# Sine angles in turns, a separate store for the first taps, and two issuers for the first Toeplitz loads

## The chip, the cores and the metric

The kernel runs on one core of one Trainium2 chip. The metric is the device time of the program in microseconds (us). The profile is of one execution of the program; its engines are called PE (TensorE, with PEld for its weight loads), DVE (VectorE), ACT (ScalarE), POOL (GpSimd) and SP (SyncE, which here only issues transfers).

## The reference, cut to what matters

Two layers run after one another on x of shape 4 x 64 x 256 x 256 (batch, channel, height, width), all in 32-bit floats.

```python
# layer 0: a long separable convolution; the filters come from small sine networks
h = sin(freq * (z @ w1 + b1))          # z: 256 positions x 33
h = sin(freq * (h @ w2 + b2))
h = sin(freq * (h @ w3 + b3))
h = (h @ wo) * decay                   # 256 taps for each of 64 channels; once for X, once for Y
k = outer product of hx and hy         # per channel
y = causal 2-D convolution of x with k # written with rfft2 of size 512
x = y + x * bias

# layer 1: whitening over the 64 channels
x1   = x as 64 x (4 * 256 * 256)
x1_s = x1[:, ::9]
cov  = x1_s @ x1_s.T / n + 0.01 * I
out  = newton_schulz_isqrt(cov, 5) @ (x1 - mean(x1_s))
```

The inputs are drawn so that the angles freq * (...) reach many turns: they have to be brought back into one turn before the sine is looked up.

## The kernel before, in words

**Filters.** The X and the Y network run together, as the two halves of 128 partitions (`wbd` holds block-diagonal weights). The 256 positions are split in two halves `u` of 128. In each of three layers `i`, a product of 128 x 128 (`pm`, L156) lands in PSUM; ACT evacuates it with scale `freq` and bias `bf` (L159); DVE brings the angle into one turn with five operations (L160 to L164: divide by 2 pi and round by adding and subtracting the constant MAGIC, take the turns off in two parts TP1 and TP2, clamp); ACT takes the sine (L165). The list `hs` feeds the next layer. After each layer's two halves, `busy(...)` puts filler products on zeros into the PE queue (L150; a call is two PE instructions, called passes in this text). A last product `pf` (L172) times `decay` (L173) gives `taps`, one row of 256 taps and 128 zeros for each of 128 filters.

**Taps to memory and back.** SP writes the first two rows to `g0_d` in memory (L174), ACT writes all 128 rows to `g_d` (L175). The Toeplitz matrix of a channel is a load in which each partition reads its row one element further on (`load_toeplitz`, L183 to L195). For the first group of 8 channels 14 such loads are issued by SP (L548 to L550), two for each piece of channels, one for each half of 64 partitions; the first pair reads `g0_d`, the rest `g_d`. The profile gives both memory tiles the name `g_d`.

**The convolution.** The work is 32 steps (a group of 8 channels of one image), each in four items of two channels. An item needs two products with Toeplitz matrices, first along one axis (read from x, copied out of PSUM to `o1`) and then along the other. `group` does the first stage of one item together with the second stage of the item two places earlier (L215, copies L399, bias L402), so the first two items run alone, in `half_group` (L247, copies L281). In it the two channels of an item begin on opposite halves of the partitions (`k = step ^ u`). Products that share row tiles are kept in order by no-operations on POOL, `fence`. Two steps ahead, SP loads x; it stores the result to `y_d` (L415), and loads further Toeplitz matrices at hand-set places (`blocks`), the first of them at step 0, c = 4. The order on every engine from here on is that of the code (`manual_schedule`).

**Sampling and whitening.** DVE packs every ninth element into `samp` (L314). The last image's last channels are packed by PE instead, with nine selection matrices `pick` (`pack_by_pe`), which POOL computes in the prologue from `ident` and `rows`, a cast of `mask` (L132 to L135). After the covariance and the Newton-Schulz steps, a second pass reads `y_d`, multiplies by the whitening matrix and writes `out` (L601 to L631).

The two writes and their fillers:

```python
    nc.sync.dma_start(out=g0_d, in_=taps[0:2])
    nc.scalar.dma_start(out=g_d, in_=taps)
    busy(20)
```

Of the kernel before, what the change touches and what calls it, by code (L numbers as in the profile page):

```python
# [37 lines left out]
F32 = mybir.dt.float32  # L38
I32 = mybir.dt.int32
AF = mybir.ActivationFunctionType  # L40
ALU = mybir.AluOpType
# [3 lines left out]
NB, C, L = 4, 64, 256  # L45
P, H2 = 128, 2
EMB, ORDER = 33, 64
PIX = L * L
CG = 8
HP = P // 2  # L50
STEP = 9
# [4 lines left out]
GW = P + L  # L56
FP = 4096


TP1 = 6.28125  # L60
TP2 = 2.0 * math.pi - TP1
MAGIC = 12582912.0


# [1 line left out]
def conv_whiten_kernel(ctx: ExitStack, tc: tile.TileContext, a: dict, out: bass.AP):  # L66
    nc = tc.nc
    x = a["x"]

    const = ctx.enter_context(tc.tile_pool(name="const", bufs=1))  # L70
# [5 lines left out]
    dram = ctx.enter_context(tc.tile_pool(name="dram", bufs=1, space=bass.MemoryType.DRAM))  # L76
# [1 line left out]

    y_d = [dram.tile([H2 * C, PIX // H2], F32, tag=f"y{n}", name=f"y_d{n}") for n in range(NB)]
    g_d = dram.tile([P, GW], F32, tag="g", name="g_d")  # L80
    g0_d = dram.tile([2, GW], F32, tag="g0", name="g0_d")

# [4 lines left out]
    cols = const.tile([P, 4], F32, tag="cols", name="cols")  # L89
    nc.scalar.dma_start(out=cols, in_=a["cols"])  # L90

    bf = const.tile([P, 3], F32, tag="bf", name="bf")
# [5 lines left out]
    mask = const.tile([P, NB, H2, STEP], I32, tag="mask", name="mask")  # L98
    bias = const.tile([P, C], F32, tag="bias", name="bias")

    def load_x(t, g, n, c):
        nc.sync.dma_start(
            out=t[:, c : c + 2],
            in_=x[n, g][:, c : c + 2],
        )
# [13 lines left out]
    ident = const.tile([P, P], F32, tag="ident", name="ident")  # L119
    make_identity(nc, ident)  # L120
    samp = []
    for n in range(NB):
        t = spool.tile([P, FP], F32, tag="samp", name=f"samp{n}")
# [5 lines left out]


    rows = const.tile([P, STEP], F32, tag="rows", name="rows")
    nc.gpsimd.tensor_copy(rows, mask[:, NB - 1, 0, :])  # L132
    pick = const.tile([P, STEP, P], F32, tag="pick", name="pick")
    for s in range(STEP):
        nc.gpsimd.tensor_scalar(pick[:, s, :], ident, rows[:, s : s + 1], None, ALU.mult)  # L135

    taps = scratch[:, 11:13, :].rearrange("p a w -> p (a w)")[:, 0:GW]
    nc.gpsimd.memset(taps[:, L:GW], 0.0)  # L140
    freq = cols[:, 3:4]
    nc.vector.tensor_scalar(bf, cols[:, 0:3], freq, None, ALU.mult)

    idle = o1pool.tile([P, H2 * L], F32, tag="o1", name="idle")
# [2 lines left out]
    def busy(times):  # L147
        p = psA.tile([P, P], F32, tag="psA", name="busy")
        for _ in range(times):
            nc.tensor.matmul(p, lhsT=idle[:, 0:P], rhs=idle[:, P : 2 * P], start=True, stop=True)  # L150

    hs, wt = [zw[:, u * P : (u + 1) * P] for u in range(2)], zw[:, L : L + P]
    for i in range(3):
        for u in range(2):
            pm = psA.tile([P, P], F32, tag="psA", name=f"pm{i}_{u}")
            nc.tensor.matmul(pm, lhsT=wt, rhs=hs[u], start=True, stop=True)  # L156
            half = slice(u * P, (u + 1) * P)
            arg, k, nxt = (scratch[:, 2 + 3 * i + v, half] for v in range(3))
            nc.scalar.activation(arg, pm, AF.Identity, bias=bf[:, i : i + 1], scale=freq)  # L159
            nc.vector.tensor_scalar(k, arg, 1.0 / (2.0 * math.pi), MAGIC, ALU.mult, ALU.add)  # L160
            nc.vector.tensor_scalar(k, k, MAGIC, None, ALU.subtract)
            for part in (TP1, TP2):
                nc.vector.scalar_tensor_tensor(arg, k, -part, arg, ALU.mult, ALU.add)  # L163
            nc.vector.tensor_scalar(arg, arg, 3.1415925, -3.1415925, ALU.min, ALU.max)  # L164
            nc.scalar.activation(nxt, arg, AF.Sin)  # L165
            hs[u] = nxt
        wt = wbd[:, i * P : (i + 1) * P]
        busy((5, 10, 9)[i])
    for u in range(2):
        half = slice(u * P, (u + 1) * P)  # L170
        pf = psA.tile([P, P], F32, tag="psA", name=f"pf{u}")
        nc.tensor.matmul(pf, lhsT=wt, rhs=hs[u], start=True, stop=True)  # L172
        nc.vector.tensor_tensor(taps[:, half], pf, decay[:, half], ALU.mult)  # L173
    nc.sync.dma_start(out=g0_d, in_=taps[0:2])  # L174
    nc.scalar.dma_start(out=g_d, in_=taps)  # L175
    busy(20)

    def new_toeplitz(g):


        return tpool.tile([P, 2, CG, L], F32, tag="toep", name=f"toep_{g}")

    def load_toeplitz(t, g, f, half, lo=0, hi=CG):  # L183
        source, row = (g0_d, 0) if (g, f, lo) == (0, 0, 0) else (g_d, f * C + g * CG + lo)


        skip = 0 if f == half else HP
        nc.sync.dma_start(
            out=t[half * HP : (half + 1) * HP, f, lo:hi, skip:],
            in_=bass.AP(  # L190
                tensor=source.tensor,
                offset=source.offset + row * GW + skip,
                ap=[[1, HP], [GW, hi - lo], [1, L - skip]],
            ),
        )  # L195
# [126 lines left out]
    def covariance(n):  # L322

        pc = psA.tile([P, C + 1], F32, tag="psA", name=f"pc{n}")
        for b in range(H2):
            for j in range(NJ):
                half = slice(C * (j % 2), C * (j % 2 + 1))
                nc.tensor.matmul(  # L328
                    pc[half],
                    lhsT=samp[n][:, b, j, 0:C],  # L330
                    rhs=samp[n][:, b, j, :],
                    start=(b == 0 and j < 2),
                    stop=(b == H2 - 1 and j >= NJ - 2),
                    skip_group_check=True,
                )
        nc.vector.scalar_tensor_tensor(cov, pc, 1.0 / NSAMP, cov, ALU.mult, ALU.add)  # L336
# [18 lines left out]
    def load_next():  # L355
        loaded[len(loaded)] = load_y(len(loaded))
# [10 lines left out]
    for g in range(1, C // CG):  # L367
        first = 16 * g - 14 if g < C // CG - 1 else 16 * g - 22
        for part in range(8):
            k = first + (part * 12 // 8 if g < C // CG - 2 else part)  # L370
# [7 lines left out]
    def pack(time=math.inf):  # L378
        while todo and time > 0:
            cost, op = todo.pop(0)  # L380
            op()
            time -= cost
# [160 lines left out]
    with tc.manual_schedule(  # L543
        engines={engines.PE, engines.SP, engines.DVE, engines.Activation, engines.Pool}
    ):
        toep = {0: new_toeplitz(0)}

        for f, lo, hi in ((0, 0, 2), (0, 2, 4), (0, 4, 6), (1, 0, 2), (0, 6, 8), (1, 2, 4), (1, 4, 8)):  # L548
            for half in range(2):
                load_toeplitz(toep[0], 0, f, half, lo, hi)  # L550
        for c in range(0, CG, 2):
            load_x(x_tiles[1], *steps[1], c)
        for i, (g, n) in enumerate(steps):
            xt = x_tiles[i % 4]
            for c in range(0, CG, 2):
                item = (g, n, c, xt, [])
                if g == C // CG - 1 and n > 0 and c == 4:
                    covariance(n - 1)
                if len(pending) == 2:
                    group(item, pending.pop(0))  # L560
                else:
                    half_group(item, 0)
                pending.append(item)
                if i == 0 and c == 6:

                    fold = const.tile([P, C], F32, tag="fold", name="fold")
                    nc.vector.tensor_tensor(fold, ident[:, 0:C], ident[:, C:P], ALU.add)

                    nc.scalar.activation(bf[:, 0:1], samp[0][:, 0, 0, C : C + 1], AF.Sqrt)

                if i + 2 < len(steps):
                    load_x(x_tiles[(i + 2) % 4], *steps[i + 2], c)
                if (i, c) in blocks:
                    tg, part = blocks[i, c]
                    if part == 0:
                        toep[tg] = new_toeplitz(tg)
                    lo = part % 2 * CG // 2
                    load_toeplitz(toep[tg], tg, part // 4, part // 2 % 2, lo, lo + CG // 2)
                for _ in range(early.get((i, c), 0)):
                    load_next()  # L580
        g, n, c, yt, _ = pending[0]
        for item in pending:
            half_group(item, 1)
            pack(1.0)
            store(item)

        pack()
        i15 = place(2 * C, rows=C).rearrange("p (u c) -> p u c", u=2)
        for u in range(2):
            nc.vector.tensor_scalar(i15[:, u], ident[0:C, 0:C], 1.5, None, ALU.mult)  # L590
        ones = place(P, rows=C)
        nc.gpsimd.memset(ones, 1.0)  # L592
        for lo in range(CG // 2, CG, 2):
            pack_by_pe(g, n, yt, slice(lo, lo + 2))
        covariance(NB - 1)
        while len(loaded) < len(homes):
            load_next()
        W, shift = whitening(i15, ones)
# [3 lines left out]
    for i, (n, q) in enumerate(pieces):  # L602
# [3 lines left out]
        part = FP if 1 < i < len(pieces) - 2 else FP // 4  # L606
        for w in range(FP // 1024):
# [5 lines left out]
            cols = [slice((2 * w + k) * 512, (2 * w + k + 1) * 512) for k in range(2)]  # L613
# [76 lines left out]
```

## Time and profile before

| what | value |
| --- | --- |
| median of 3 runs | 910.22 us (907.89 to 911.49) |
| profiled execution, its own time | 911.4 us |
| its span, first to last instruction | 909.6 us |
| mean granted PE clock | 0.951 |
| first product of the convolution that is followed by an unbroken stream | 19.44 us |
| POOL: nine picks | 5.46 us, from 11.80 |
| SP: 14 first Toeplitz loads | issued from 15.23 to 25.85 us |

A row of the page or of the timeline names line, engine, operation and tiles. In the timeline the first number is the start in us from the first instruction, the second the duration of the merged instructions, `x4` their number, and in brackets the idle time before them with what ended it. In the chain of waits there are start, duration and what the time was spent on; "issue" is time in which the engine waited for nothing that is shown, `SPq` SP's queue. A row of the table by stretch gives the stretch, its length, the busy time (and the number of instructions) of PE, PEld, DVE, ACT and POOL, then the granted PE clock, the mean busy share of the 16 DMA engines and GB/s.

### The profile page before, as it was taken

What the parts mean: (1) busy time and instruction counts of PE and PEld (TensorE: products, weight loads), DVE (VectorE), ACT (ScalarE), POOL (GpSimd) and SP (SyncE); (2) the same over time, 40 slices, a digit from 0 to 9 for tenths busy, and PEclk for the clock granted to TensorE, in tenths of its full rate; (3) what the DMA queues carried; (4) which work ended last, traced back from release to release, by engine and by line L of the source; (5) the groups of instructions that cost most, each with busy time, mean ns of one, the idle gap of its engine ahead of it and who ended that gap; (6) DMA issues with size and microseconds to landing.
All of it is one profiled execution on the core that took longest, in us unless ns stands there. A gap on an engine that the chain in (4) does not pass through costs nothing.

```text
span 909.6 us, 28286 instructions
## 1 busy us (share of the span) xinstructions
PE 792.2 (87%) x11928; PEld 636.7 (70%) x11928; DVE 657.6 (72%) x882; ACT 479.8 (53%) x798; POOL 31.4 (3%) x71
## 2 busy tenths in 40 slices
PE   8999999999999999999999999999977777775500
PEld 7999999999999999999999999998411111111100
DVE  3368786878687868876787766767699999996500
ACT  2545454545454545555555544541598888885400
POOL 3000000000000000000000000000110000000010
PEclk9999999999999999999999999998999999996655
DMA  4998788797888788878987898879899999999998
GB/s 154 303 305 261 250 243 263 251 276 247 253 262 265 247 255 267 263 249 253 297 282 234 285 400 323 290 253 386 346 383 433 428 432 429 428 433 428 432 430 342
DMA packets 117550, 285.61 MB, mean 314 GB/s; under 512 B 8973, under 2 KB 91312, under 8 KB 109744
## 3 DMA queue, kind: packets, MB, share of 16 engines
q1 hardware_dynamic: 110800, 216.49, 70.1%
q0 software_dynamic: 6336, 67.11, 17.4%
q8 instruction: 95, 1.56, 0.7%
q14 instruction: 31, 0.25, 0.1%
q10 hardware_dynamic: 288, 0.20, 0.1%
HBM read 149.35 MB, written 134.42 MB: 312 GB/s over the span
## 4 chain that ended last, share of the span: by engine, by line
PE 68%; DVE 15%; issue 14%; DMA 1%; POOL 0%; ACT 0%; POOLq 0%; SPq 0%; DVEq 0%; ACTq 0%
PE p L215 64%; DVE yi L624 13%; PE pc L328 2%; PE ph L247 1%; DVE samp L314 1%; PE busy L150 1%; POOL out_dram L629 0%; PE po L616 0%; DMA toep<-g_d 0%; DVE x L284 0%; PE spin L429 0%; PE pm L156 0%; DMA scratch<-in_zw_dram 0%; DMA g_d<-scratch 0%; DVE scratch L163 0%
## 5 line engine op out<-in xcount | busy, mean ns | idle before, releaser
L215 PE MATMUL p<-toep,x 64*64 64x64 f32 (+3 forms) x5040 | 578.5, 284 | 0.0
L215 PE MATMUL p<-toep,o 64*64 64x64 f32 (+3 forms) x5040 | 578.5, 284 | 0.0
L215 PEld LDWEIGHTS p<-toep,x 64*128 64x128 f32 (+1 forms) x5040 | 534.3, 166 | 23.4 <-issue 0.3
L215 PEld LDWEIGHTS p<-toep,o 64*128 64x128 f32 (+1 forms) x5040 | 535.2, 166 | 10.3
L399 ACT COPY o<-p 64x512 f32<-64x512 f32 x504 | 292.2, 580 | 296.0 <-PE p L215 288.5
L314 DVE COPY_PREDICATED samp<-mask,x 128x448 f32<-128x448 int32 (+3 forms) x288 | 281.0, 976 | 6.7
L402 DVE SCALAR_TENSOR_TENSOR x<-x,bias,p 128x512 f32<-128x512 f32 x252 | 177.3, 743 | 138.9 <-PE p L215 138.5
L624 DVE TENSOR_SCALAR yi<-po,shift 64x512 f32<-64x512 f32 x256 | 192.1, 750 | 22.2 <-PE po L616 16.0
L616 PE MATMUL po<-yi,chain 64*64 64x512 f32 x1024 | 152.7, 668 | 59.9 <-DVE yi L624 41.7
L621 ACT ACTIVATE yi<-po,shift 64x512 f32<-64x512 f32 x256 | 174.8, 683 | 38.9 <-PE po L616 31.4
L616 PEld LDWEIGHTS po<-yi,chain 64*64 64x64 f32 x1024 | 35.9, 145 | 175.7 <-DVE yi L624 129.6
L629 POOL DMA_DIRECT2D out_dram<-yi x44 | 23.6, 537 | 256.0 <-DVE yi L624 155.0
L592 POOL MEMSET chain<- 64x128 f32 x1 | 0.2, 198 | 603.0 <-PE ph L247 603.0
L328 PE MATMUL pc<-samp 128*64 128x65 f32 x464 | 17.3, 243 | 2.0 <-ACT samp L304 2.0
L328 PEld LDWEIGHTS pc<-samp 128*64 128x64 f32 x464 | 16.8, 155 | 3.2 <-ACT samp L304 2.2
L150 PE MATMUL busy<-idle 128*128 128x128 f32 x88 | 12.3, 304 | 0.0
L150 PEld LDWEIGHTS busy<-idle 128*128 128x128 f32 x88 | 11.9, 219 | 0.2 <-issue 0.2
L336 DVE SCALAR_TENSOR_TENSOR cov<-pc,cov 128x65 f32<-128x65 f32 x4 | 0.9, 226 | 14.7 <-PE pc L328 14.7
L281 DVE COPY o<-ph 64x256 f32<-64x256 f32 x8 | 3.4, 422 | 9.5 <-PE ph L247 9.4
L281 ACT COPY o<-ph 64x256 f32<-64x256 f32 x8 | 2.9, 366 | 10.4 <-PE ph L247 10.3
L295 PE MATMUL pk<-x,pick 128*128 128x56 f32 (+1 forms) x72 | 8.3, 292 | 0.0
L295 PEld LDWEIGHTS pk<-x,pick 128*128 128x128 f32 x72 | 8.1, 192 | 0.1
(92 smaller groups left out, 84.4 us busy)
## 6 DMA issues: line engine op xcount, KB each, us to landing
x<-in_x_dram SPq DMA_DIRECT2D x128, 512.0 KB, 5.6
y_d<-x SPq DMA_DIRECT2D x256, 256.0 KB, 4.2
yi<-y_d SPq DMA_DIRECT2D x32, 2048.0 KB, 15.1
out_dram<-yi POOLq DMA_DIRECT2D x28, 2048.0 KB, 43.2
out_dram<-yi POOLq DMA_DIRECT2D x16, 512.0 KB, 9.5
toep<-g_d SPq DMA_DIRECT2D x29, 256.0 KB, 6.4
toep<-g_d SPq DMA_DIRECT2D x29, 192.0 KB, 6.4
toep<-g_d SPq DMA_DIRECT2D x6, 128.0 KB, 3.0
```

Source lines behind the costliest of these rows:

```text
L150: nc.tensor.matmul(p, lhsT=idle[:, 0:P], rhs=idle[:, P : 2 * P], start=True, stop=True)
L215: mm = nc.tensor.matmul(ps[q : q + w, m, HP * k : L], lhsT=src[parts, k // 2, m * P + q : m * P + q + w], rhs=t[parts, : stop : -1] if k e ...
L247: mm = nc.tensor.matmul(ps[m][:, HP * k : L], lhsT=src[parts, k // 2, m * P : (m + 1) * P], rhs=t[parts, : stop : -1] if k else t[parts, : ...
L295: nc.tensor.matmul(pk[:, b, :, 0:nj], lhsT=pick[:, (s - b) % STEP, :], rhs=yt[:, cs, b, s : s + STEP * (nj - 1) + 1 : STEP], start=(s == 0 ...
L314: nc.vector.copy_predicated(dst, m, src)
L328: nc.tensor.matmul(pc[half], lhsT=samp[n][:, b, j, 0:C], rhs=samp[n][:, b, j, :], start=(b == 0 and j < 2), stop=(b == H2 - 1 and j >= NJ ...
L399: nc.scalar.copy(o1[to], units[u][0][0][fr])
L402: nc.vector.scalar_tensor_tensor(x2[:, c2 + u], x2[:, c2 + u], bias[:, ch : ch + 1], units[u][1][0], ALU.mult, ALU.add,)
L616: nc.tensor.matmul(po[u][halves[k]], lhsT=W[halves[u]], rhs=yt[halves[u], cols[k]], start=True, stop=True,)
L621: nc.scalar.activation(yt[halves[0], cols[k]], po[0][halves[k]], AF.Identity, bias=shift[halves[k]])
L624: nc.vector.tensor_scalar(yt[halves[1], cols[k]], po[1][halves[k]], shift[halves[k]], None, ALU.add)
L629: nc.gpsimd.dma_start(out=o[:, end - part : end], in_=yt[:, end - part : end])
```

## The change

The angles are kept in turns. `freq` is divided by 2 pi once, by a new DVE operation ahead of `bf`, so that `arg` is in turns; rounding is one addition of MAGIC; one operation, (k - MAGIC) - arg, gives the negative of the remainder; the sine takes it with scale -TURN. Two DVE operations remain of five. For the first half, the evacuation of PSUM goes from ACT to DVE. The filler counts fall from 5, 10, 9 and 20 to 2, 4, 4 and 16.

`g0_d` now holds the taps of all 8 first channels of both filters, in two writes, one by SP and one by ACT; the write of `g_d` goes to POOL. All loads of group 0 read `g0_d`, and those of the second half of the partitions are issued by ACT.

The cast of `mask` is moved behind POOL's write, and the nine `pick` products go from POOL to ACT, three after each of the first three groups of step 1.

```diff
-TP1 = 6.28125
-TP2 = 2.0 * math.pi - TP1
+TURN = 6.283185
...
-    g0_d = dram.tile([2, GW], F32, tag="g0", name="g0_d")
+    g0_d = dram.tile([2 * CG, GW], F32, tag="g0", name="g0_d")
...
     rows = const.tile([P, STEP], F32, tag="rows", name="rows")
-    nc.gpsimd.tensor_copy(rows, mask[:, NB - 1, 0, :])
     pick = const.tile([P, STEP, P], F32, tag="pick", name="pick")
-    for s in range(STEP):
-        nc.gpsimd.tensor_scalar(pick[:, s, :], ident, rows[:, s : s + 1], None, ALU.mult)
+
+    def load_pick(lo, hi):
+        for s in range(lo, hi):
+            nc.scalar.activation(pick[:, s, :], ident, AF.Copy, scale=rows[:, s : s + 1])
...
-    freq = cols[:, 3:4]
+
+    freq = const.tile([P, 1], F32, tag="freq", name="freq")
+    nc.vector.tensor_scalar(freq, cols[:, 3:4], 1.0 / (2.0 * math.pi), None, ALU.mult)
     nc.vector.tensor_scalar(bf, cols[:, 0:3], freq, None, ALU.mult)
...
-            nc.scalar.activation(arg, pm, AF.Identity, bias=bf[:, i : i + 1], scale=freq)
-            nc.vector.tensor_scalar(k, arg, 1.0 / (2.0 * math.pi), MAGIC, ALU.mult, ALU.add)
-            nc.vector.tensor_scalar(k, k, MAGIC, None, ALU.subtract)
-            for part in (TP1, TP2):
-                nc.vector.scalar_tensor_tensor(arg, k, -part, arg, ALU.mult, ALU.add)
-            nc.vector.tensor_scalar(arg, arg, 3.1415925, -3.1415925, ALU.min, ALU.max)
-            nc.scalar.activation(nxt, arg, AF.Sin)
+            if u == 0:
+                nc.vector.tensor_scalar(arg, pm, freq, bf[:, i : i + 1], ALU.mult, ALU.add)
+            else:
+                nc.scalar.activation(arg, pm, AF.Identity, bias=bf[:, i : i + 1], scale=freq)
+
+            nc.vector.tensor_scalar(k, arg, MAGIC, None, ALU.add)
+            nc.vector.scalar_tensor_tensor(arg, k, MAGIC, arg, ALU.subtract, ALU.subtract)
+            nc.scalar.activation(nxt, arg, AF.Sin, scale=-TURN)
             hs[u] = nxt
         wt = wbd[:, i * P : (i + 1) * P]
-        busy((5, 10, 9)[i])
+        busy((2, 4, 4)[i])
...
-    nc.sync.dma_start(out=g0_d, in_=taps[0:2])
-    nc.scalar.dma_start(out=g_d, in_=taps)
-    busy(20)
+    nc.sync.dma_start(out=g0_d[0:CG], in_=taps[0:CG])
+    nc.scalar.dma_start(out=g0_d[CG:], in_=taps[ORDER : ORDER + CG])
+    nc.gpsimd.dma_start(out=g_d, in_=taps)
+    nc.gpsimd.tensor_copy(rows, mask[:, NB - 1, 0, :])
+    busy(16)
...
-    def load_toeplitz(t, g, f, half, lo=0, hi=CG):
-        source, row = (g0_d, 0) if (g, f, lo) == (0, 0, 0) else (g_d, f * C + g * CG + lo)
+    def load_toeplitz(t, g, f, half, lo=0, hi=CG, issue=nc.sync):
+        source, row = (g0_d, f * CG + lo) if g == 0 else (g_d, f * C + g * CG + lo)
...
-        nc.sync.dma_start(
+        issue.dma_start(
...
-                load_toeplitz(toep[0], 0, f, half, lo, hi)
+                load_toeplitz(toep[0], 0, f, half, lo, hi, nc.scalar if half else nc.sync)
...
+                if i == 1 and c < CG - 2:
+                    load_pick(c // 2 * 3, c // 2 * 3 + 3)
```

## The prediction

> **What bounds the kernel now.** I read the page first, for which engine the span belongs to.
>
> ```profile
> PE 792.2 (87%) x11928; PEld 636.7 (70%) x11928; DVE 657.6 (72%) x882; ACT 479.8 (53%) x798; POOL 31.4 (3%) x71
> PE   8999999999999999999999999999977777775500
> DMA  4998788797888788878987898879899999999998
> ```
>
> TensorE fills 27 slices (22.7 us each), and then the transfers fill the rest. The busy table by stretch confirms this at both ends: from 52 to 600 us TensorE is busy for 547.96 of 548 us, and from 700 us the DMA is saturated.
>
> ```profile
> 52.00:600.00 548.00, 547.96 (x9670) 515.67 (x9668) 416.82 (x505) 273.63 (x472) 0.00 (x0) 1.00 0.85 270
> 700.00:780.00 80.00, 57.36 (x416) 11.53 (x412) 77.59 (x104) 70.51 (x105) 6.39 (x12) 1.00 1.01 429
> ```
>
> The change touches neither stretch. It touches what lies ahead of the first Toeplitz product, so I read the chain of waits from 0 to 60 us next.
>
> ```profile
> 6.24 0.85 PE pm L156 x4
> 7.09 2.84 PE busy L150 x20
> 9.93 0.24 PE pm L156 x2
> ...
> 13.66 0.30 DVE scratch L173
> ...
> 14.03 1.18 DMA g_d<-scratch
> ...
> 15.23 0.68 SPq L188
> ...
> 15.95 3.35 DMA toep<-g_d
> 19.30 0.14 issue
> 19.44 5.83 PE ph L247 x55
> 25.26 34.82 PE p L215 x615
> ```
>
> Everything before 19.44 is a serial prologue: three sine layers, the taps (ready at 13.96), a 3 KB write, and two loads. From 19.44 on TensorE never waits for a transfer until the whitening. What is cut from the prologue therefore moves the whole stream, then the whitening, then the transfers that can only start with the whitening matrix. I count it one to one.
>
> **Part 1: the sine layers.** The timeline gives the pieces. A layer's first product to its ScalarE start takes 0.83 us in layer 1 (2.59 to 3.42), 0.68 in layer 2 (6.03 to 6.71) and 0.43 in layer 3 (9.77 to 10.20). ACT L159 takes 0.46, DVE L160 and L161 0.23 each, L163 0.28, L164 0.23, ACT L165 0.31. A DVE operation starts 0.26 after the one that it depends on, and an engine change costs 0.05. Layer starts are 2.59, 6.03, 9.77, and the write of the taps is issued at 14.03.
>
> The change removes three of five DVE operations per half, and for half 0 also the ScalarE evacuation, which becomes a DVE operation reading PSUM. That form is not in the trace; it is bounded by L142 (0.23) and L173, which reads PSUM (0.29). I take 0.29, the nearer. Half 0 now needs 0.30 + 0.26 + 0.28 + 0.05 + 0.31 + 0.05 = 1.25 us from result to next product. The extra DVE operation for freq (0.23, row L142) ends with its successor at 2.82 + 0.26 + 0.23 = 3.31, ahead of the first result at 3.42, so it costs nothing; if cols landed later, at most 0.26.
>
> - Layer 1: 3.42 + 1.25 = 4.67. But the next product needs the wbd weights, issued at 1.22 and landing 3.9 us later by the DMA view: 5.12. The next late thing takes over 0.5 us of the gain. Layer 2 starts at 5.2 instead of 6.03.
> - Layer 2: 5.2 + 0.68 + 1.25 = 7.13 by the sines. The filler products in the same queue may be later: 4 passes of the products and 8 of busy(4). Here a rule of the skill matters.
>
> ```profile
> 3.74 2.50 PE L150 MATMUL busy<-idle 128*128 128x128 f32 x10
> 13.46 4.63 PE L150 MATMUL busy<-idle 128*128 128x128 f32 x40
> ```
>
> Early fillers run at about 0.21 us a pass, late ones at 0.11; the narrow timeline puts the switch near 7.9 us, 5.3 us after the first product. At 0.21 the 12 passes take 2.55 us and hold layer 3 until 7.75. The Trainium skill ("TensorE: Matmul & The Clock Gate", What's actually happening) says that the array runs at half clock until one window of about 3.4 us was busy, and that the window runs free. By that rule the switch comes anywhere from 6.0 to 9.4; at 6.0 there is no overrun. By the row the overrun is 0.62, by the rule's early end 0. I take half: layer 3 starts at 7.45 (7.13 to 7.75).
> - Layer 3 and taps: the result takes 0.43 to 0.68; I take 0.55. Half 1 keeps ScalarE: 7.45 + 0.55 + 0.22 (two passes) + 0.46 = 8.68, then DVE 0.06 + 0.26 + 0.28, 0.05, the sine 0.31, 0.05: product at 9.69. Product to taps was 13.13 to 13.66, 0.53; L173 0.29; to issue 0.08. The write is issued at 10.59. With busy(4) at 0.21 a pass throughout there would be another 0.6 us.
>
> 14.03 - 10.59 = 3.44 us saved: 0.83 in layer 1, 1.49 in layer 2, 1.12 in layer 3.
>
> **Part 2: taps out, Toeplitz in.** Before, issue of the small write to first steady product took 19.44 - 14.03 = 5.41 us. In it the second half waited 0.72 us for SP to issue the first (15.23 to 15.95), and TensorE needs both halves, since the two channels of the first pair start on opposite halves. Now SP and ACT write 12 KB each. The nearest row is the 3 KB write at 1.18; the 192 KB write by ACT took 4.1. I take 1.2, being 8 rows against 2 and far from 128. Then both halves are issued at once: 0.05 + 1.2 + 0.02 + 3.0 (the page's median landing of these loads; 2.8 to 3.35 are the ends) + 0.14 = 4.41. Saved: 1.0 us.
>
> A rule speaks against this part: the Trainium skill ("DMA: Bandwidth & Descriptors", Issuing engines are not separate DMA queues) says that several issuers share the same 16 engines and save only issue time. If the pair shared them fully, the second half would land as late as before, and the saving would be 0.3. But from 18 to 20 us the DMA share was only 0.27 to 0.30, so there is room, and the issue time is exactly what stood in the chain. I take the row.
>
> The other 12 loads: SP issued all 14 by 25.85; now 7 each at 0.63 us are out by about 16.3. They are not waited for before or after. ACT pays 7 x 0.63 = 4.4 us, from 11.9 to 16.3; its next work, the copies of L281, began 2.6 us after TensorE's start, so at about 17.6. Covered by 1.3 us. The loads of x behind them on SP go out earlier. The large g_d write moves to POOL: nearest rows 4.1 (ACT, 192 KB) and 9.5 (POOL, 512 KB). Its first reader is the load seen at 33.84, about 29 now, 18 us after the issue: free. On POOL itself, ahead of the fences between row tiles, it costs 0.5 to 0.7 (rows of L629) plus a 0.21 cast, over 3 us before the first fence.
>
> **Part 3: the picks.** POOL's nine products (5.46 us) go to ACT, three after each of three groups of step 1. Nearest row L165, 0.31; L159 says 0.46. So 0.9 to 1.4 us a group, where the next copy waits for TensorE anyway:
>
> ```profile
> 42.92 2.39 ACT L399 COPY o<-p 64x512 f32<-64x512 f32 x4 [1.57 <-PE p L215]
> 48.13 2.37 ACT L399 COPY o<-p 64x512 f32<-64x512 f32 x4 [2.83 <-PE p L215]
> ```
>
> Cost zero; uncovered it would delay a copy by some tenths, and the banks of one more group lie between that and TensorE. Left on POOL, the picks (to 17.26) would have met the earlier fences.
>
> **Sum.** 3.44 + 1.0 = 4.4 to 4.5 us. The profiled execution took 911.4 us (span 909.6), 1.2 above the median of the runs shown; from the median 910.2, minus 4.5, I forecast 905.7. About 0.5%, 4.55 us, is what a measurement here tells from no change, so the sum lies on that bound.
>
> **Rivals.**
> - *The clock at the start of the stream.* busy(16) is 32 passes, 3.6 us at full clock, ending near 13.5, against products from 15.0. Before, the gap to the first product was about 0.4 us; now 1.5. Were the array throttled for one 3.4 us window, 1.7 us would be lost: 907.4, no measurable change. Against: the gap is under half a window.
> - *The prologue is held elsewhere.* Fillers or late weights hold each layer, and only one layer's saving and the split issue remain, some 2 us: 908.2. The chain's own filler piece at 7.09 speaks for it, the smaller counts against.
> - *Slower: ACT is caught behind its transfers.* ACT's queue is in order, and it holds 7 loads ahead of the copies that TensorE needs. If an issue has to wait for an earlier landing, each costs more than 0.63. The queue's own waits show this for SP between 31 and 40 us (L188 behind x loads, 1.8 us in two). At t us each, the copies are late by 7t - 5.7: nothing below 0.81, all the gain gone at 1.46, and at a full landing of 3.0 us TensorE waits 15 us: 921. Against: SP issued 14 such loads without one wait of this kind.
>
> **How the numbers follow.** The sum holds: 0.80; with about 1.3 us of spread between medians, and small gains that I left out (L163 no longer stretched to 0.38 beside POOL's picks), 0.48 of it beyond the bound and 0.32 within. Clock: 0.05, within. Held elsewhere: 0.05, within, but 0.02 of it beyond. ACT caught: 0.10, slower. So faster 0.50, same 0.40, slower 0.10. The sum's ends: no overrun, 0.43 and 2.8 give a saving of 5.1; full overrun in both layers, 0.68 and 3.35 give about 3.0. With the spread of the runs (907.9 to 911.5), and the two middle rivals, the range is 902.6 to 909.0.
>
> **What would show it.** Right: the tap write issued near 10.6, first steady product near 15.0, second layer's product just behind the wbd landing at 5.1, no TensorE wait in the stream, and the stream's length unchanged. Wrong: a landing of the first loads over 3.4 us, fillers ahead of a layer's product in the chain, L281 late on ACT, granted clock under 1.00 around 15 to 20 us, or a shift at the start that is not found again at the end.

## The result, and the profile after

The median of 22 runs is 908.33 us (906.85 to 910.18), that of the kernel before, in 22 runs beside it, 910.16. The medians differ by 1.8 us. The ratio, estimated from all the runs, is 0.9976, with a 95% interval from 0.9966 to 0.9986: 0.24% of 910, about 2.2 us less, where 4.5 were forecast. It is clear of noise, and less than half of what was expected. The profiled execution of the changed kernel took 907.4 us (span 905.3).

First the page of the changed kernel, the lines that answer to those shown of before: busy time of the engines, and PE and DMA in 40 slices.

```profile
PE 784.6 (87%) x11892; PEld 630.5 (70%) x11892; DVE 656.2 (72%) x868; ACT 481.5 (53%) x804; POOL 26.4 (3%) x63
PE   8999999999999999999999999999977777765500
DMA  7988779788788788888997899879999999999998
```

PE has 7.6 us less busy time, with 36 passes fewer, as many as there are fillers fewer; DVE has 14 instructions fewer. Nothing has changed in the picture of the stages: the table by stretch of the changed kernel shows a TensorE that is never free from 52 to 600 us, and the same transfer rate at the end.

```profile
52.00:600.00 548.00, 547.85 (x9688) 514.71 (x9686) 417.15 (x505) 273.31 (x473) 0.00 (x0) 1.00 0.85 269
700.00:780.00 80.00, 57.38 (x416) 11.71 (x416) 77.56 (x105) 70.70 (x104) 6.38 (x12) 1.00 1.01 429
```

The difference lies in the prologue. This is its chain of waits after the change, from 0 to 60 us.

```profile
2.57 1.22 PE pm L157 x4
3.79 1.15 PE busy L151 x4
4.95 1.13 PE pm L157 x4
6.07 1.29 PE busy L151 x8
7.36 0.24 PE pm L157 x2
...
10.04 0.30 DVE scratch L175
...
10.41 1.39 DMA g_d<-scratch
11.80 0.02 issue
11.82 4.06 DMA toep<-g_d
15.88 0.14 issue
16.02 7.31 PE ph L251 x56
23.33 36.81 PE p L219 x637
```

Read it against the chain of before. The write of the taps is issued at 10.41 instead of 14.03: 3.6 us won, and 10.59 was forecast. But the first unbroken products start at 16.02 instead of 19.44: only 3.4 left, not 4.4. And the last two lines hold the surprise: the two half groups, on which nothing was changed, take 7.31 us instead of 5.83. The full groups start at 23.33 instead of 25.26, 1.9 us earlier.

The table by stretch says what happened in these 7.31 us. Its columns are the same as before; the one to look at is the granted clock, third from the end. First the changed kernel, in two stretches of 3.41 us; the second is the time at half clock.

```profile
13.57:16.98 3.41, 1.64 (x12) 1.29 (x13) 0.00 (x0) 0.00 (x0) 0.00 (x0) 1.00 0.88 215
16.98:20.39 3.41, 3.41 (x27) 3.36 (x25) 0.45 (x2) 0.65 (x2) 0.00 (x0) 0.50 0.99 214
```

And the kernel before, over its own half groups.

```profile
19.44:25.26 5.82, 5.82 (x64) 5.64 (x66) 1.87 (x5) 1.79 (x5) 0.00 (x0) 1.00 0.58 166
```

In a stretch of 3.4 us, PE was busy for 1.64; in the next 3.4 us its clock was 0.50, where before it was 1.00 throughout. Half of 3.4 us at half clock is 1.7 us of work undone; the half groups took 1.5 us longer.

### The profile page after: what moved, and what is told of

The parts are those of the page before. It is cut to its first block, busy times and chain, and to the rows that moved or that the text cites. A ratio compares the mean times of both kernels' runs of the same rounds, so it can differ in the third digit from the quotient of the medians.

```text
span 905.3 us, 28200 instructions
## 1 busy us (share of the span) xinstructions
PE 784.6 (87%) x11892; PEld 630.5 (70%) x11892; DVE 656.2 (72%) x868; ACT 481.5 (53%) x804; POOL 26.4 (3%) x63
## 4 chain that ended last, share of the span: by engine, by line
PE 68%; DVE 16%; issue 9%; DMA 5%; POOL 0%; ACT 0%; POOLq 0%; DVEq 0%; SPq 0%; ACTq 0%
PE p L219 63%; DVE yi L630 14%; DMA yi<-y_d 3%; PE pc L332 2%; DVE samp L318 1%; DMA out_dram<-yi 1%; PE ph L251 1%; PE po L622 1%; DMA toep<-g_d 0%; POOL out_dram L635 0%; DVE x L288 0%; DVE x L406 0%; ACT yi L627 0%; PE pm L157 0%; PE spin L433 0%
## 5 line engine op out<-in xcount | busy, mean ns | idle before, releaser
L622 PE MATMUL po<-yi,chain 64*64 64x512 f32 x1024 | 149.7, 652 | 61.7 <-DVE yi L630 42.2
L251 PE MATMUL ph<-toep,x 64*128 64x192 f32 (+3 forms) x64 | 8.0, 391 | 1.8 <-DMA toep<-g_d 1.8
L251 PEld LDWEIGHTS ph<-toep,x 64*128 64x128 f32 x64 | 7.2, 234 | 2.5 <-issue 1.5
```

The source lines that it names most:

```text
L251: mm = nc.tensor.matmul(ps[m][:, HP * k : L], lhsT=src[parts, k // 2, m * P : (m + 1) * P], rhs=t[parts, : stop : -1] if k else t[parts, : ...
L622: nc.tensor.matmul(po[u][halves[k]], lhsT=W[halves[u]], rhs=yt[halves[u], cols[k]], start=True, stop=True,)
```

## The experiments

Two questions: why does the load part give nothing, and does the clock explain the half groups? The start of the full groups in one profile shows a part's effect to a tenth of a microsecond; the ratios speak for many executions, but with intervals of some 1 to 2 us either way.

**More last fillers.**

```diff
-    busy(16)
+    busy(24)
```

> Only the last filler count goes from 16 to 24, so that PE works until about 15.2 us instead of 13.6, and the first loads land at 15.9 as before. Theory 1 (the PE clock was halved for one 3.4 us window because PE stood almost idle between 13.6 and 16.0): no half-clock window after the first product, the two half groups take 5.8 us instead of 7.3, and the median falls by 1 to 1.5 us against the changed kernel, to about 907. Theory 2 (the half groups are slow because their later loads land late, or because the copies are late): they still take about 7.3 us at full clock and the time stays at 908.3.

Median 908.73, ratio to the kernel before 0.9974 (0.9965 to 0.9983). In the profile PE works until 15.95, the clock stays at 1.00, and the half groups take 6.03 us: the chain of waits of this kernel ends so.

```profile
12.41 4.01 DMA toep<-g_d
...
16.55 6.03 PE ph L251 x59
22.58 37.60 PE p L219 x645
```

For the profile, theory 1 holds. The median did not fall by the expected 1 us, so the ratio alone doesn't show it: the half-clock window costs its 1.5 us only in some executions (below; in two of five it would be 0.6 us, less than these intervals can tell), and the tap write of this profile came late, at 11.01.

**Fewer last fillers, the suspected cost doubled.**

```diff
-    busy(16)
+    busy(8)
```

> The full change with 8 instead of 16 last fillers, so that PE stands idle from about 11.7 to 15 us and nearly idle to 16. Theory 1 (idle PE costs a half-clock window): the half-clock stretch comes in the profile whatever the phase, 3.4 us or 6.8 us long, the half groups take 7.3 us or more, and the median is 0.5 to 2 us above the full change, 909 to 910.5. Theory 2 (the fillers do nothing): half groups as in the full change, and the same time.

Median 910.73, ratio 1.0012 (0.9999 to 1.0025): the whole gain of the change is gone, somewhat more than theory 1 said. The half groups take 9.02 us in the profile, at a mean clock of 0.67:

```profile
15.12:24.14 9.02, 9.01 (x66) 8.15 (x68) 1.88 (x5) 1.79 (x5) 0.00 (x0) 0.67 1.00 247
```

These fillers compute on zeros and nobody reads them. Eight calls fewer cost 3.3 us against the changed kernel in ratio (1.0012 - 0.9976 = 0.36%; with both intervals some 1.8 to 4.8 us). So the cost of idle PE is shown over many executions; that it is paid through the clock is seen in the profile, where the clock was 0.50 from 14.23 to 21.06.

**All loads on SP.**

```diff
-                load_toeplitz(toep[0], 0, f, half, lo, hi, nc.scalar if half else nc.sync)
+                load_toeplitz(toep[0], 0, f, half, lo, hi)
```

> All 14 loads are issued by SP again, the rest of the change stays. The prediction's step (both halves at once save the 0.72 us of issue): the first steady product comes 0.7 us later than with two issuers, at 16.7, and the time rises by 0.7. Rival (nothing was gained by the second issuer): the product stays at 15.9 to 16.1, with the second half landing 3.3 us after its own issue at 12.5, and the time is that of the changed kernel within 0.5 us.

Median 907.7, ratio 0.9967 (0.9955 to 0.9979), no worse than with two issuers. In its chain the first half lands 3.11 us after its issue, at 15.38; the second, issued at 13.00, lands 3.07 us after that. The first products run at 15.51, and steady ones at 16.20, which is 3.93 us after 12.27; with two issuers that was 4.20 (11.82 to 16.02).

```profile
12.27 3.11 DMA toep<-g_d
...
15.51 0.68 PE ph L251 x2
16.20 5.82 PE ph L251 x55
22.03 38.18 PE p L219 x651
```

So the prediction's step is refuted: there was no 0.72 us to be had from the second issuer.

**The first pair by two engines, the rest by SP.** The issuer is ACT only `if half and (f, lo) == (0, 0)`.

> Only the first pair of loads is issued by two engines; the other 12 are issued by SP one after the other. Theory 1 (the first pair lands late because the 12 loads behind it share its engines): the second half lands about 3.0 to 3.4 us after issue instead of 4.1, and the first steady product comes 0.7 to 1.0 us earlier, at about 15.2. Theory 2 (two loads issued at once are served one after the other in any case): it lands at about 4 us still, and the product stays near 16.0. The time moves by less than 1 us either way.

Median 907.95, ratio 0.9967 (0.9958 to 0.9977). The second half lands 3.96 us after its issue though the other twelve loads are now issued one by one: theory 2, then. (This profile, too, has a half-clock window, and half groups of 7.31 us.) The transfers' view by short stretches shows the order of service. Here is the changed kernel itself, what moved from 13.2 to 13.8 and from 14.4 to 15.0 us; q1 is SP's queue, q10 ACT's, then packets, MB and share.

```profile
q1 hardware_dynamic: 87, 0.08, 42.7%
...
q10 hardware_dynamic: 80, 0.06, 79.8%
q1 hardware_dynamic: 45, 0.04, 19.6%
```

Both loads were issued at 11.8. From 13.2 to 13.8 only SP's moves, on DMA engines that are less than half busy. ACT's first packet starts at 14.05, when 119 of SP's 128 KB have started.

**Issuers exchanged.** `nc.sync if half else nc.scalar`.

> The halves change issuers: ACT issues the loads of the first 64 partitions, SP those of the second. Theory 1 (what ACT issues is served late, some 0.7 to 1 us behind SP): the first half now lands at about 4.1 us after issue and the second at about 3.0 to 3.5; products start at the same time, about 16.0. Theory 2 (the second half lands late whoever issues it, because of where it goes): the second half still lands at 4.1 and the first at 3.0.

The single time, 907.9 us, says nothing by itself. The view of transfers, cut to the moment of the first two issues, has size and time from issue to landing; this is the exchanged kernel.

```profile
toep<-g_d ACTq DMA_DIRECT2D x1, 128.0 KB, 3.8
toep<-g_d SPq DMA_DIRECT2D x1, 96.0 KB, 2.8
```

And the changed kernel.

```profile
toep<-g_d SPq DMA_DIRECT2D x1, 128.0 KB, 3.0
toep<-g_d ACTq DMA_DIRECT2D x1, 96.0 KB, 4.1
```

In these two it is ACT's load that lands a microsecond later, not the second half: theory 1. But ACT is not always second. In the profile with 24 last fillers, the same two loads, issued as in the changed kernel, landed the other way round.

```profile
toep<-g_d SPq DMA_DIRECT2D x1, 128.0 KB, 4.0
toep<-g_d ACTq DMA_DIRECT2D x1, 96.0 KB, 3.5
```

In all seven profiles with such a pair the first packet of one load starts 0.3 to 0.9 us after that of the other: six times ACT's is the later, here SP's. What sets the order was not tried. The products wait for both: steady ones start 3.91 us after the issue in the exchanged kernel (12.18 to 16.09). Here the clock stays at 1.00, with the same 16 fillers.

**One part at a time: the sine layers alone.** The kernel before, with the sine lines, `freq` and fillers (2, 4, 4) of the change, and all else as it was:

```diff
-        busy((5, 10, 9)[i])
+        busy((2, 4, 4)[i])
```

> The kernel before with only the sine layers of the change and their filler counts (2, 4, 4); stores, loads, picks and the last 20 fillers as before. Theory 1 (all of the gain is the shorter sine chain, the load part gives none): taps written at 10.4 to 11.0, loads as before 5.4 us behind, first steady product near 16.2; POOL's picks, still ending near 17.3, hold the first fences by about 1 us; the time falls by 2 to 3 us, as in the full change. Theory 2 (the load part does its share): the time falls by 1 us less than in the full change.

Median 907.83, ratio 0.9964 (0.9951 to 0.9978). The taps are written at 11.00; the old 3 KB write and the loads on SP bring the first product at 15.23:

```profile
11.00 1.18 DMA g_d<-scratch
...
12.20 2.90 DMA toep<-g_d
...
15.23 6.45 PE ph L248 x57
21.68 38.41 PE p L216 x650
```

The sine part alone is no worse than the whole change. I had expected POOL's picks, busy until 17.1, to hold the first fences by 1 us; the half groups give no sign of it (6.45 us from the first product, against 6.52 with all loads on SP and no picks there).

**The other part alone.** The changed kernel with the old sine lines and the old fillers (5, 10, 9 and 20).

> The full change without its sine part: old angles, old filler counts (5, 10, 9 and 20), but new stores, two issuers, and picks on ACT. The prediction's step: first steady product 4.4 us after the tap write instead of 5.4, and 1 us less time. Theory 1 (no gain from the loads): 5.4 to 5.6 us, and the time within 0.5 us of the kernel before.

Median 910.42, ratio 1.0003 (0.9989 to 1.0017): nothing that can be told, where 1.0 us was forecast. From tap write to full groups it is 10.87 us (13.47 to 24.34) in its profile, with 20 fillers and full clock, against 11.23 before: 0.4 us less.

**Both kernels once more.** The unchanged files, for a second profile each.

> The kernel before once more, for one profile: no half-clock window near the first products, since its fillers end 0.4 us before them; the tap write between 13.4 and 14.6 us, according to when the full clock is granted, and full groups from 24.4 to 25.9.

> The changed kernel once more, for one profile: where the windows of the clock lie against the idle stretch from 13.6 to 16.0 decides. Either a half-clock window of 3.4 us and half groups of 7.3 us, as in the first profile, or full clock and half groups of 5.8 to 6.1 us, with full groups from about 22.1; tap write at 10.4 to 11.0 in both.

The kernel before: tap write at 13.38, full groups at 24.71, and full clock from 6.85 on, through the half groups. The changed kernel: tap write at 10.69, and this time no half-clock window near the first products, though the stretch from 13.57 has as little work in it (1.65 us of PE). The half groups:

```profile
16.28:22.10 5.82, 5.82 (x64) 5.64 (x66) 1.87 (x5) 1.79 (x5) 0.00 (x0) 1.00 1.00 208
```

So the same gap costs 1.5 us in one execution and nothing in the next. Of the five profiles with 16 fillers after the new sines (the changed kernel twice, loads on SP, first pair on two engines, issuers exchanged) two have the half-clock window.

The traces say where the windows lie. Within each of the 14 profiles all changes of the granted clock are whole multiples of 3.413 us apart (in the changed kernel 6.77, 17.01, 20.43, 628.00 and so on), and this grid lies differently against the program in each execution: the first full clock came between 6.77 and 9.06. So each profile can be cut along its own grid, and the window that holds the gap can be compared with the clock of the window after it. In the changed kernel that window runs from 13.60 to 17.01, with 1.66 us of PE in 12 products, and the next ran at 0.50. The four others, in the order of their start: first pair on two engines (next window at 0.50), changed kernel again, issuers exchanged, and loads on SP (next window at 1.00 in these three).

```profile
13.91:17.32 3.41, 1.93 (x15) 1.59 (x16) 0.00 (x0) 0.00 (x0) 0.00 (x0) 1.00 0.76 208
14.23:17.64 3.41, 2.02 (x15) 1.68 (x16) 0.00 (x0) 0.00 (x0) 0.00 (x0) 1.00 0.90 232
14.40:17.81 3.41, 1.72 (x17) 1.62 (x18) 0.00 (x0) 0.00 (x0) 0.00 (x0) 1.00 1.02 248
14.63:18.04 3.41, 2.50 (x20) 2.13 (x21) 0.00 (x0) 0.00 (x0) 0.00 (x0) 1.00 0.69 174
```

Ordered by the number of products, 12 and 15 were followed by half clock, and 15, 17 and 20 were not; with 8 last fillers 11 products were (10.82 to 14.23). Busy time does not order them: 1.93 us was followed by half clock and 1.72 was not. So in these profiles the place of the grid decides: the later the window begins, the more of the useful products fall into it. What exactly is counted these runs do not show, and no run moves the grid on purpose.

**Towards a better version.** First, the change with its weak points mended: all loads on SP, and

```diff
-        busy((2, 4, 4)[i])
+        busy((2, 2, 4)[i])
...
-    busy(16)
+    busy(26)
```

> The full change with all 14 loads on SP, 26 last fillers, and the fillers after layer 2 cut from 4 to 2. Theory 1: no half-clock window at the start, no filler in front of layer 3's product, tap write at 10.2 to 10.6, first products at about 3.2 us and steady ones at 3.9 us behind the loads' issue, the stream's full groups from about 21.6; the median 907.0 or less, 3 to 3.5 us below the kernel before. Theory 2 (these terms are within what varies anyway): 907.7 to 908.5.

Median 907.33, ratio 0.9963 (0.995 to 0.9976). The fillers no longer stand before layer 3, but 26 at the end are too many: the chain goes from filler to product without a wait, and the full groups start at 22.07, hardly earlier than in the changed kernel's second profile (22.10).

```profile
10.28 5.81 PE busy L151 x52
16.09 5.98 PE ph L251 x58
22.07 38.01 PE p L219 x649
```

Then the same with 22 fillers and the first pair cut by channel, in the order of use:

```diff
+        for half, lo, issue in ((0, 0, nc.sync), (1, 1, nc.scalar), (1, 0, nc.sync), (0, 1, nc.scalar)):
+            load_toeplitz(toep[0], 0, 0, half, lo, lo + 1, issue)
-        for f, lo, hi in ((0, 0, 2), (0, 2, 4), (0, 4, 6), (1, 0, 2), (0, 6, 8), (1, 2, 4), (1, 4, 8)):
+        for f, lo, hi in ((0, 2, 4), (0, 4, 6), (1, 0, 2), (0, 6, 8), (1, 2, 4), (1, 4, 8)):
```

> All loads on SP, 22 last fillers, 2 fillers after layer 2, and the first pair of loads cut into four of one channel each, issued in the order in which the products use them: channel 0 first half and channel 1 second half first, on SP and on ACT. Theory 1 (loads issued at once by two engines are served one after the other, so what counts is how much stands in front): both of the first two land some 0.5 us earlier than the two-channel pair, the steady products begin 3.2 to 3.5 us after the loads' issue instead of 3.9 to 4.2, and the time is at or up to 0.5 us below the kernel with loads on SP and 26 fillers. Theory 2 (a fixed latency and contention with the 192 KB write set the landing): 3.9 us or more as before.

Median 907.43, ratio 0.9957 (0.9941 to 0.9974). Steady products start 3.1 us after the issue (12.11 to 15.21), and full groups at 21.32, the earliest of all. With less in front of it, what is served second lands earlier (ACT's first load 2.82 us after its issue), as theory 1 has it; but the loads are also half as large, which is not told apart, and the products here came straight behind the fillers, so that the loads may have been in time for an earlier start.

Last, the old stores and loads on SP with the new sines, the picks on ACT, and fillers 2, 2, 4 and 20:

> The kernel before with the sine layers of the change, fillers 2, 2, 4 and 20, and the picks on ACT; the taps stored as before (two rows by SP, all by ACT) and all loads on SP. Theory 1 (the sine part is the whole gain, and the old stores and loads are as good as the new): tap write near 10.6, full groups from about 21.4 to 21.8, 3.3 to 3.7 us less time than the kernel before. Rival (the new stores and loads give a share): 1 us slower than the kernel with the full change, loads on SP and 26 fillers.

Median of 6 runs 906.34, beside 911.24 of the kernel before: ratio 0.9938 (0.9919 to 0.9958). The full groups start at 21.55. It beats the kernel before and, in its interval, the changed kernel. From the two variants above it is not told apart: the intervals overlap, and its start lies between theirs (22.07 and 21.32). Its 5.6 us are more than the 3.7 by which its full groups start earlier; the rest has no counterpart in the prologue and stays open.

## Why the prediction was half right

**The stage, and the one-to-one transfer: right.** In the 14 profiles, span less start of the full groups lies between 882.0 and 884.9 us, with no clear relation to the start, which itself ranges over 3.9 us (before 884.3 and 883.4; changed 882.0 and 882.5). What the prologue wins arrives at the end, within that spread.

**Part 1, the sine layers: right in mechanism, a little large.** Forecast 3.44 us. The two profiles before wrote the taps at 14.03 and 13.38, the two of the changed kernel at 10.41 and 10.69: 3.2 us between the means. The profile I worked from was the slower of the two: the full clock came at 8.23 us in it and at 6.85 in the other, and its filler passes stayed slow longer. In the first profile of the changed kernel it came at 6.77, the earliest of all. So the 3.6 us between the first two profiles, more than forecast, are in part luck; with the full clock at nearly the same time (6.85 and 6.77) it is 3.0. In the pieces:
- The DVE operation that reads PSUM, bounded at 0.23 to 0.29, takes 0.41 us.
- Layer 2's products started at 4.80, not at 5.2: the weights, taken to land at 5.12, did not hold them.
- The sine that layer 3 needs ended at 6.97 (ACT, 6.66 and 0.31); fillers held its product until 7.20. Forecast was 7.45, with half an overrun.

```profile
3.41 0.41 DVE L161 TENSOR_SCALAR scratch<-pm,freq,bf 128x128 f32<-128x128 f32 x1 [0.20 <-PE pm L157]
7.20 0.84 PE L157 MATMUL pm<-scratch 128*128 128x128 f32 x4
```

**Part 2, the loads: the step that failed.** Forecast: both halves issued at once land 3.0 us later, 1.0 us saved. Measured from tap write to full groups: before 11.23 and 11.33 us; changed, at full clock, 11.41. Nothing was saved, 0.1 us was lost. From tap write to steady products it took 5.61 us, not 4.41. Two terms of the sum were too small. The larger write landed after 1.39 us instead of the 1.2 I took. And the second half landed after 4.06 us, where 3.0 was taken: that is 0.72 + 3.35 = 4.07 of before, as if it were still issued second. The prediction also says that with fully shared engines 0.3 us would be saved; a second half as late as before gives 0.05 + 1.2 + 0.02 + 4.07 + 0.14 = 5.48 in its own terms, which is none. I weighed the sentence in the Trainium skill ("DMA: Bandwidth & Descriptors", Issuing engines are not separate DMA queues), that issuing from several engines saves only issue time, against a DMA share of 0.27 to 0.30 and took the row. The sentence spoke rightly against the step, and the failure goes further than it says: issue time was saved, since 14 loads by two issuers took 6.5 us (0.93 each on ACT) against 10.05 by SP alone (0.72 each), but none of it reached the products. DMA engines with room to spare did not mean that a second load was served at once: it began 0.3 to 0.9 us after the first. Why it did stays open. And the share of 0.27 to 0.30 was read from 18 to 20 us, when the first load's packets were through; from 16.6 to 17.4, while they moved, it was 0.54.

The 0.1 us hides two larger parts, for the loads of before did not stay the same once the sines were shorter. With the new sines the old stores and loads took 10.68 and 10.79 us from tap write to full groups (the sines alone, and the last variant), not 11.23 and 11.33. Against these the new ones lose 0.6 to 0.7 us. In both profiles before, the write of `g_d` landed after 4.1 us, and after 1.9 with the sines alone; a transfer of 16 KB of instructions (queue q8 of the transfers' view, 1.6 us in one packet from 15.19) ran beside it in the first case (in the other profile before: 1.9 us from 14.31), and only at 18.03 in the second.

```profile
q8 instruction: 1, 0.02, 1.8%
...
g_d<-scratch ACTq DMA_DIRECT2D x1, 192.0 KB, 4.1
```

```profile
g_d<-scratch ACTq DMA_DIRECT2D x1, 192.0 KB, 1.9
```

That this transfer slowed the first loads of before (3.35 us for the second half, 2.80 with the sines alone) fits, but no run moved it alone.

**The clock: the rival that I gave 0.05.** "Were the array throttled for one 3.4 us window, 1.7 us would be lost": it was, and 1.5 us was lost, in two profiles of five. The argument against it, that the gap is under half a window, missed that the loads landed 1 us later than forecast, so that the gap ran on to 16.0; only 0.67 us of products lay in it. The two errors were one: what made the loads late opened the gap. The Trainium skill ("TensorE: Matmul & The Clock Gate", HAM oscillation) puts the limit at idle gaps of about 3.4 us. Here 1.75 us without work in a window of 3.41 were enough, and 1.69 in another execution (issuers exchanged) were not; the measurement goes beyond the rule.

**Sum.** 3.2 us from the sines, less 0.1 from tap write to full groups, less 1.5 where the window falls in: 1.6 us in one execution and 3.1 in another. The measured 2.2 (1.3 to 3.1, from the interval) lies between.

**The rest held.** The write of `g_d` from POOL landed after 2.3 us and nobody waited for it. The picks take 0.33 each on ACT, 0.99 for three, and the next copy still waits 0.55 us for PE. ACT's loads occupied it until 18.3, not 16.3: over the 0.81 us each from which I said copies would be late. Since the products started late as well, the copies at 19.73 were not held. That cover is 1.4 us, a margin which an earlier start would have used up.

```profile
11.82 6.48 ACTq L192 DMA_DIRECT2D toep<-g_d  x7
39.53 0.99 ACT L134 ACTIVATE pick<-ident,rows 128x128 f32<-128x128 f32 x3
41.06 2.39 ACT L403 COPY o<-p 64x512 f32<-64x512 f32 x4 [0.55 <-PE p L219]
```

## What to carry to other kernels

When a chain is shortened, count again the work that was there to fill its gaps: filler products that are cut in proportion leave a gap as soon as one term of the chain doesn't shrink, and the half clock can then fall on the first useful products. Before giving a second engine half of a row of loads, do not take room on the DMA engines for service at once: here two loads issued together were served with a lag, and only a trial of one issuer against two told it. And test the parts of a composite change alone: here one part carried the gain, and the other carried none. Such parts need not add up: here the loads took another time once the sines were shorter.

## What the runs showed of the hardware that was not expected

- Two loads of 96 and 128 KB in rows of 768 and 1024 bytes, issued within 0.01 us by SP and ACT, were not served together: in seven profiles the first packet of one started 0.3 to 0.9 us after that of the other, while the DMA engines were less than half busy (42.7% from 13.2 to 13.8 us in the changed kernel). ACT's was the later in six of them, SP's in one.
- The changes of the PE clock lie on a grid of 3.413 us in each of the 14 profiles. A window of this grid in which PE was busy for 1.66 us, and one with 1.93 us, were followed by a window at 0.50; others with 1.72, 2.02 and 2.50 us were not. With fillers that end at 12.03 us and the first product at 15.12, two windows ran at 0.50, and the half groups took 9.02 us instead of 5.82.
- A DVE operation on 128 x 128 elements in PSUM with two per-partition operands took 0.41 us; one of the same kind on SBUF with constants took 0.23. Which of the two differences costs the time was not tried.
- A transfer of 16 KB of instructions took 1.6 and 1.9 us as one packet beside the tap writes of the kernel before, and the 192 KB write there landed after 4.1 us instead of 1.9; whether the one causes the other is open.
